# Side work of an expert stream: four lanes with gaps and a VectorE allowance, norms scaled on ScalarE, choices block by block

## The chip, the core and the metric

One core of a Trainium2 chip. The time is that of the device, in microseconds (us), for one execution of the whole kernel. The engines are TensorE (PE in the profile), VectorE (DVE), ScalarE (ACT), GpSimd (POOL) and SyncE (SP), which here only issues DMAs. Each engine executes its own instructions in their order.

## What is computed

Everything is float32; x has four sequences of 1024 rows of 256. The reference, cut to its frame:

```python
x = x + attention(layernorm(x))      # 16 heads, rotary, q and k normed, (q.k)**4, causal
x = x + ffn(layernorm(x))
x = x + silu(conv(layernorm(x)))     # long convolution along the axis of the 4 sequences: 4 taps
x = x + ffn(layernorm(x))            # the same weights again

def ffn(x):
    shared = (silu(x @ g) * (x @ u)) @ w2s                 # inner width 352
    probs = softmax(x @ gate_w.T)                          # 16 experts
    weights, chosen = top_k(probs, 6)
    return shared + sum(weights[k] * expert[chosen[k]](x)) # inner width 176
```

## The kernel before

All of x stays in SBUF as `X`, eight blocks of 128 positions by four sequences. The blocks form two groups of four. A first part does attention, and in its second half the routing of group 0. Then an expert stream runs in four stages: group 0 and group 1 through the first feed-forward layer, then the same through the second. A stage streams 111 tiles, each of 128 rows that one expert takes; which expert it is stands in `table`.

Around a stage lie two steps on GpSimd, both of indirect DMAs with 128 rows each, 96 per group and layer. The *scatter* (`scatter`, L421) writes the normed rows (`sxn`) into a queue in DRAM (`xq`), at places that `plan` worked out. The stage loads the queue three tiles at a time (`xg`, L1001), and stores its results in a second queue (`yq`, L1064). The *combine* (`combine`, gathers at L1147) fetches them back into `yg`, and VectorE adds them to `X`, weighted with the softmax's values `top` (L1131).

One tile of the stream is: `turn` (TensorE transposes the rows, `pxt`, L1014; ScalarE copies them to `xgT`, L1016), `gate_up` (L1030; ScalarE's silu L1038 and VectorE's product L1039 give `hbuf`), `turn_h` (L1044, L1046) and `down` (L1053; ScalarE copies `py` to `yo`, L1062). `stream` writes them out so that one round of its loop holds `gate_up` of tile c, `turn_h` of c - 2, `turn` of c + 2 and `down` of c - 3. After `down` it calls the stage's function with the number of the tile.

That function hands out side work. A piece of side work is a generator that yields "el" or "pe" ahead of a portion (a bite; "pe" ones use TensorE) or "gap" (wait for the next round). `Bites` keeps lanes of such generators, and `step` runs so many bites of each lane. The order is fixed when the program is built, since TensorE, VectorE, ScalarE and SyncE are scheduled by hand; GpSimd's instructions stay in the order in which they were written. In the stream there are three lanes, and gaps are skipped:

- QUEUE: the combine of the previous stage's group, one pair of gathers a tile; when it and SIDE are empty, the scatter for the next stage (one a tile in stage 0, every eighth tile two; two a tile in stages 1 and 2). Each scatter is made to follow the last copy of `hT` written before it.
- SIDE: of each block that the combine completed, `convolve` (norm, four taps, silu, sum), `prepare` (norm, logits) and, after the fourth block, `plan` (softmax, the best eight, one-hot `hot` and its sum `mask`, places `sloti`, and `table` by way of `le` and `ex`). Stage 0 has `prepare` and `plan` of group 1, without `convolve`.
- FILL: the shared expert of the stage's group (28 bites, one every fourth tile).

If a stage's rows are wanted while its scatter is unfinished, `force` drains all side work ahead of them:

```python
def run():
    settle()
    if st not in filled:
        bites.add(QUEUE, fill(st, 2))
        settle()
```

Stage 3 combines group 0 for the last time, three gathers every second tile. After the stream, a tail combines group 1 in triples, each with one bite of the shared expert, and stores the blocks.

Of the kernel before, what the change touches and what calls it, by code (L numbers as in the profile page):

```python
# [8 lines left out]
FP = mybir.dt.float32  # L9
# [15 lines left out]
P = 128  # L25
# [19 lines left out]
class Bites:  # L45
# [4 lines left out]
    def __init__(self, lanes, gaps=True):  # L50
        self.lanes = [[] for _ in range(lanes)]
        self.gaps = gaps

    def add(self, lane, gen, key=None):
        self.lanes[lane].append([key, gen, None])
        self.advance(lane, -1)

    def advance(self, lane, at):
        item = self.lanes[lane][at]
        item[2] = next(item[1], None)  # L60
        while item[2] == "gap" and not self.gaps:
            item[2] = next(item[1], None)
        if item[2] is None:
            self.lanes[lane].pop(at)
# [13 lines left out]
    def step(self, pe, counts):  # L78

        for lane, n in enumerate(counts):  # L80
            for _ in range(n):
                kind = self.kind(lane)
                if kind in (None, "gap") or (kind == "pe" and pe <= 0):
                    break
                if kind == "pe":
                    pe -= 1
# [17 lines left out]
def block_kernel(  # L104
# [25 lines left out]
    rt2 = ctx.enter_context(tc.tile_pool(name="rt2", bufs=2))  # L130
    dram = ctx.enter_context(tc.tile_pool(name="dram", bufs=1, space=bass.MemoryType.DRAM))
# [39 lines left out]
    iota_i = rt.tile([P, NTILE], I32, name="iota_i")  # L171
    nc.gpsimd.iota(iota_i, pattern=[[1, NTILE]], base=0, channel_multiplier=0)
    iota_f = rt.tile([P, NTILE], FP, name="iota_f")
    nc.vector.tensor_copy(iota_f, iota_i)
    iota_e = iota_f[:, 0:NEXP]
    row0 = rt.tile([1, NTILE], FP, name="row0")
    nc.vector.tensor_scalar_mul(row0, iota_f[0:1, :], float(P))
# [8 lines left out]
    def ln_stats(xs, mv, tag):  # L186

        st = small.tile([P, 4, 6], FP, tag=f"st_{tag}", name="ln_st")
        for i in range(4):
            nc.vector.bn_stats(st[:, i, :], xs[:, i, :])  # L190
        for i in range(4):
# [5 lines left out]
    def ln_apply(xs, dst, mv, rstd, n=4):  # L197

        for i in range(n):
# [3 lines left out]
                mv[:, i, 0:1],  # L203
                rstd[:, i : i + 1],
                ALU.subtract,
                ALU.mult,
            )
# [44 lines left out]
    mvs = [rt.tile([P, TT, 2], FP, name=f"mvs{g}") for g in range(NG)]  # L252
    rstds = [rt.tile([P, TT], FP, name=f"rstds{g}") for g in range(NG)]
    plans = {}
    logits = {}
    scatters = [0]

    def prepare(g, i, pool, ps):

        t = g * TG + i  # L260
        xs = X[:, t, :, :]
        mv, rstd = mvs[g][:, 4 * i : 4 * i + 4, :], rstds[g][:, 4 * i : 4 * i + 4]
        yield "el"
        if i == 0:
            logits[g] = rt.tile([P, TT, NEXP], FP, name="lg")
        lg = logits[g]
        ln_stats(xs, mv, "r")
# [5 lines left out]
        nc.vector.reciprocal(rstd, rstd)  # L273
        xn = pool.tile([P, 4, E], FP, tag="rxn", name="rxn")
        ln_apply(xs, xn, mv, rstd)
        xT = pool.tile([P, 2, 512], FP, tag="rxT", name="rxT")
        yield "gap"
        yield "gap"
        for k in range(2):
# [4 lines left out]
        yield "gap"  # L284
# [11 lines left out]
        nc.vector.tensor_copy(lg[:, 4 * i : 4 * i + 4, :], pl)  # L296

    def plan(g, ps):

        yield "el"  # L300
        lg = logits[g]
        sh3 = [P, TT, NEXP]
        mx = small.tile([P, TT], FP, tag="mx", name="mx")
        nc.vector.tensor_reduce(mx, lg, AX.X, ALU.max)
        nc.vector.tensor_sub(lg, lg, mx[:, :, None].to_broadcast(sh3))
        yield "gap"
        yield "el"
        nc.scalar.activation(lg, lg, AF.Exp)
        yield "gap"
        yield "el"  # L310
        sm = small.tile([P, TT], FP, tag="smx", name="smx")
        nc.vector.tensor_reduce(sm, lg, AX.X, ALU.add)
        nc.vector.reciprocal(sm, sm)
        nc.vector.tensor_mul(lg, lg, sm[:, :, None].to_broadcast(sh3))

        top = rt2.tile([P, TT, 8], FP, name="top")
        idx = rt.tile([P, TT, 8], U32, name="idx")
        for c in range(0, TT, 8):
            yield "el"
            for i in range(c, c + 8):  # L320
                nc.vector.max(top[:, i, :], lg[:, i, :])
            for i in range(c, c + 8):
                nc.vector.max_index(idx[:, i, :], top[:, i, :], lg[:, i, :])
        yield "el"
        chosen = rt.tile([P, TT, TOPK], FP, name="chosen")
        nc.vector.tensor_copy(chosen, idx[:, :, 0:TOPK])
        hot = rt.tile([P, TT, TOPK, NEXP], FP, name="hot")
        sh4 = [P, TT, TOPK, NEXP]
# [6 lines left out]
        yield "el"  # L335
        mask = rt.tile([P, TT, NEXP], FP, name="mask")
        nc.vector.tensor_reduce(mask, hot.rearrange("p t k n -> p t n k"), AX.X, ALU.add)

        mf = mask.rearrange("p t n -> p (t n)")
        yield "gap"  # L340
        yield "gap"
        yield "pe"
        pa = ps().tile([P, TT, NEXP], FP, tag="m", name="pa")
# [4 lines left out]
        nc.vector.tensor_copy(tot[:, :, 0:TT], pa.rearrange("p t n -> p n t"))  # L348
        cnt = small.tile([P, NEXP], FP, tag="cnt", name="cnt")
# [19 lines left out]
        yield "el"  # L369
        nc.vector.tensor_mul(hot, hot, at[:, :, None, :].to_broadcast(sh4))  # L370
# [950 lines left out]
```

## Time and profile before

| | us |
|---|---|
| median of 3 runs (2469.45 to 2477.04) | 2473.38 |
| the profiled execution | 2393.24 |
| its span, first to last instruction | 2391.5 |
| TensorE busy in it | 2114.5 (88%) |
| VectorE / ScalarE / GpSimd busy | 1118.5 / 1240.2 / 901.4 |
| granted TensorE clock, mean | 0.925 |

The first `yo` of the stages start at 862.0, 1179.1, 1583.6 and 1989.7 us, the last `yo` of all at 2260.1. The page's slices are 59.8 us each; a digit gives the tenths of a slice in which the engine was busy. A row of waits names the instruction that waited, what it waited for, the sum in us, how often, and the longest. A row of the timeline has start, length, engine, line and operands, and in brackets the idle time ahead of it with what ended it. A row of windows has for each engine the busy time and the instructions in that stretch; when asked for one line of the kernel, only for that line's.

### The profile page before, as it was taken

To read this page: it belongs to the slowest core of one execution; us is meant where nothing else is said; L and a number is where in the kernel's file an instruction comes from. 1 tells how busy PE (TensorE), PEld (TensorE's weight loads), DVE (VectorE), ACT (ScalarE), POOL (GpSimd) and SP (SyncE) were. 2 spreads that over 40 slices of the span, in tenths; PEclk is the share of its full clock that TensorE was granted. 3 is DMA by queue.
4 is the path that set the end of the run, shared out by engine and by line. 5 is a ranking of instruction groups with operands and counts; after the bars stand their busy time and mean duration, and the time that the engine had idled before them with its cause. 6 is when DMAs were issued, how large, how long until landed. Compare 5 with 4: busy or idle time off the path is not lost.

```text
span 2391.5 us, 33033 instructions
## 1 busy us (share of the span) xinstructions
PE 2114.5 (88%) x10480; PEld 1308.4 (55%) x10480; DVE 1118.5 (47%) x2532; ACT 1240.2 (52%) x2754; POOL 901.4 (38%) x990
## 2 busy tenths in 40 slices
PE   5899999778898998999899999789999959999974
PEld 2344443222233466777666667567676747777632
DVE  5888867656555225111166652126754212441154
ACT  3677878566676145555455544335553424555410
POOL 3333211344431000444355226645513654540176
PEclk8888988889888999999999999989999979999987
DMA  7900000111101412555455335344423535663243
GB/s 232 342 7 1 1 1 1 38 51 45 53 27 62 114 48 79 165 166 166 137 151 154 102 104 176 132 139 142 145 92 121 176 124 154 202 186 115 91 123 112
DMA packets 212231, 267.73 MB, mean 112 GB/s; under 512 B 25280, under 2 KB 187232, under 8 KB 212064
## 3 DMA queue, kind: packets, MB, share of 16 engines
q1 hardware_dynamic: 166944, 161.04, 21.6%
q0 software_dynamic: 36992, 100.78, 13.4%
q10 hardware_dynamic: 8128, 3.80, 0.7%
q8 instruction: 91, 1.49, 0.3%
q14 instruction: 76, 0.62, 0.1%
HBM read 123.72 MB, written 141.82 MB: 111 GB/s over the span
## 4 chain that ended last, share of the span: by engine, by line
PE 67%; DVE 12%; issue 7%; ACT 7%; POOL 5%; DMA 2%; ACTq 0%; POOLq 0%; DVEq 0%; SPq 0%
PE pgu L1030 20%; PE py L1053 14%; PE ps L694 6%; PE acc L742 4%; PE pxt L1014 4%; PE pht L1044 4%; POOL xq L421 3%; PE pg L955 3%; ACT s L705 3%; PE pj L571 3%; PE pu L955 3%; PE po L972 3%; POOL yg L1147 2%; ACT s L863 1%; DVE X L1131 1%
## 5 line engine op out<-in xcount | busy, mean ns | idle before, releaser
L421 POOL DMA_INDIRECT xq<-sxn,sloti x384 | 379.2, 987 | 644.7 <-ACT xgT L1016 306.2
L1030 PE MATMUL pgu<-wgu,xgT 128*128 x1776 | 609.7, 466 | 4.4 <-DVE hbuf L1039 2.2
L1147 POOL DMA_INDIRECT yg<-yq,sloti x384 | 375.8, 979 | 421.8 <-issue 201.4
L1039 DVE TENSOR_TENSOR hbuf<-hbuf,pgu 128x176 f32<-128x176 f32 x444 | 149.4, 337 | 721.7 <-ACT hbuf L1038 721.2
L1030 PEld LDWEIGHTS pgu<-wgu,xgT 128*128 128x128 f32 x1776 | 338.7, 193 | 136.5 <-issue 20.3
L1038 ACT ACTIVATE hbuf<-pgu 128x176 f32<-128x176 f32 x444 | 141.4, 318 | 411.7 <-PE pgu L1030 411.6
L705 ACT ACTIVATE s<-ps 128x1024 f32<-128x1024 f32 (+3 forms) x384 | 291.4, 815 | 114.6 <-PE ps L694 113.5
L1053 PE MATMUL py<-w2a,hT 128*128 x888 | 268.7, 385 | 0.9 <-ACT yo L1062 0.9
L1053 PE MATMUL py<-w2b,hT 128*128 x888 | 266.4, 382 | 0.0
L1062 ACT COPY yo<-py 128x256 f32<-128x256 f32 x444 | 166.1, 374 | 167.0 <-PE py L1053 166.7
L1131 DVE SCALAR_TENSOR_TENSOR X<-yg,top,X 128x256 f32<-128x256 f32 x384 | 186.0, 484 | 87.8 <-DMA yg<-yq,sloti 81.8
L1014 PE MATMUL pxt<-ident,xg 128*128 128x128 f32 x888 | 171.8, 276 | 60.6 <-DMA xg<-xq 60.6
L714 POOL TENSOR_SCALAR_AFFINE_SELECT s<-s 128x256 f32<-128x256 f32 x128 | 84.2, 659 | 349.7 <-ACT s L705 349.5
L725 DVE TENSOR_TENSOR s<-s 128x1024 f32<-128x1024 f32 (+3 forms) x160 | 168.2, 1051 | 86.8 <-ACT s L705 83.5
L1016 ACT COPY xgT<-pxt 128x256 f32<-128x256 f32 x444 | 167.9, 378 | 68.7 <-PE pxt L1014 68.3
L694 PE MATMUL ps<-q,kA 32*128 32x512 f32 (+3 forms) x1024 | 182.0, 647 | 20.0 <-ACT s L705 18.0
L1044 PEld LDWEIGHTS pht<-ident,hbuf 128*128 128x128 f32 x888 | 125.9, 142 | 124.4 <-issue 71.1
L1053 PEld LDWEIGHTS py<-w2b,hT 128*128 128x128 f32 x888 | 170.2, 192 | 23.5
L863 ACT ACTIVATE s<-s 128x1024 f32<-128x1024 f32 x192 | 164.4, 856 | 27.5 <-POOL s L714 27.2
L1044 PE MATMUL pht<-ident,hbuf 128*128 128x128 f32 x888 | 171.6, 275 | 4.9 <-ACT hT L1046 4.9
L1046 ACT COPY hT<-pht 128x256 f32<-128x256 f32 x444 | 165.4, 372 | 1.7 <-PE pxt L1014 0.7
L742 PE MATMUL acc<-s,vA 128*32 128x512 f32 (+3 forms) x1024 | 140.1, 603 | 13.2 <-ACT s L863 10.8
(158 smaller groups left out, 2421.9 us busy)
## 6 DMA issues: line engine op xcount, KB each, us to landing
xg<-xq SPq DMA_DIRECT2D x148, 384.0 KB, 3.7
yq<-yo SPq DMA_DIRECT2D x148, 384.0 KB, 2.8
xq<-zero SPq DMA_DIRECT2D x74, 384.0 KB, 4.6
xq<-sxn,sloti POOLq DMA_INDIRECT x384, 2.4
yg<-yq,sloti POOLq DMA_INDIRECT x384, 2.9
wgu<-in_w SPq DMA_DIRECT2D x4, 1408.0 KB, 17.8
X<-in_x SPq DMA_DIRECT2D x8, 512.0 KB, 5.5
out<-X SPq DMA_DIRECT2D x8, 512.0 KB, 3.5
```

The source lines that it names most:

```text
L421: d = nc.gpsimd.indirect_dma_start(out=xq[g][:, :], out_offset=bass.IndirectOffsetOnAxis(ap=sloti[:, c + i, k : k + 1], axis=0), in_=xs[:, ...
L694: nc.tensor.matmul(tiles[h // 2][:, h % 2, 0:nq], lhsT=kt[32 * h : 32 * h + 32, (j % 4) * P : (j % 4 + 1) * P], rhs=qT[u, hf][a][32 * h : ...
L705: nc.scalar.activation(s2[:, :, 0:nq], tiles[pr][:, :, 0:nq], AF.Square)
L725: nc.vector.tensor_mul(part, part, part)
L742: nc.tensor.matmul(acc[32 * r : 32 * r + 32, n0:512], lhsT=va[:, j % 4, h * VW : h * VW + 32], rhs=s2s[r // 2][:, r % 2, 0 : 512 - n0], st ...
L863: nc.scalar.activation(part, part, AF.Square)
L1014: nc.tensor.transpose(pt[:, k, :], xg[c][:, k * P : (k + 1) * P], ident)
L1030: nc.tensor.matmul(pg, lhsT=xT[c][:, k, :], rhs=wgu_f[k][:, bass.ds(vals[0] * (2 * FI), 2 * FI)], start=(k == 0), stop=(k == 1),)
L1044: nc.tensor.transpose(pt[:, k, :], hbuf[c % 4][:, k * P : (k + 1) * P], ident)
L1053: nc.tensor.matmul(py, lhsT=hT[c][:, k, :], rhs=w2_f[k][:, bass.ds(off[c] * E, E)], start=(k == 0), stop=(k == 1),)
L1131: nc.vector.scalar_tensor_tensor(X[:, t, l, :], yg[:, k, :], top[:, i, k0 + k : k0 + k + 1], X[:, t, l, :], op0=ALU.mult, op1=ALU.add,)
L1147: nc.gpsimd.indirect_dma_start(out=yg[:, k, :], out_offset=None, in_=yq[g][:, :], in_offset=bass.IndirectOffsetOnAxis(ap=sloti[:, i, k0 + ...
```

## The change

- `Bites` keeps the gaps in the stream, too. A bite may carry a VectorE time in us; a `step` has an allowance (`room`), and a bite with a time isn't begun once it is used up. Overdraft carries over to the next step, what is left over does not.
- There are four lanes: QUEUE, CONV (convolutions of a group's blocks), CHOOSE (norm, logits and choice of each block, then the plan) and FILL. The stage's function is called twice a tile, before and after `down`, with an allowance of 1.2 each. CONV and CHOOSE share one square root for a block's first norm and the previous block's second.
- Norms in the stream are applied as scale and shift by ScalarE (`ln_apply_act`): for `hxn`, `rxn`, `hn` and `sxn`. In the attention part they stay on VectorE.
- The best eight, `hot` and `mask` are worked out block by block in `choose`, from the logits; the softmax follows after the plan. `table` comes from one comparison with a number per partition and a matmul with the identity.
- The scatter starts when the plan has its places: two a tile in stage 0, three a tile in stages 1 and 2.
- The combine goes in pairs with four buffers everywhere (`f4`), in stages 1 and 2 three pairs in two tiles; also in the tail, where each pair has one bite of the shared expert.
- `hbuf` has three buffers instead of four.

```diff
 class Bites:
-    def __init__(self, lanes, gaps=True):
+    def __init__(self, lanes):
         self.lanes = [[] for _ in range(lanes)]
-        self.gaps = gaps
+        self.room = 0.0
...
-    def step(self, pe, counts):
+    def step(self, pe, counts, room=1e9):
+        self.room = room + min(self.room, 0.0)
         for lane, n in enumerate(counts):
             for _ in range(n):
                 kind = self.kind(lane)
                 if kind in (None, "gap") or (kind == "pe" and pe <= 0):
                     break
+                time = self.lanes[lane][0][3]
+                if time > 0 and self.room <= 0:
+                    break
+                self.room -= time
...
+    def ln_scale_shift(mv, rstd, shift):
+        nc.vector.reciprocal(rstd, rstd)
+        nc.vector.scalar_tensor_tensor(
+            shift, mv[:, :, 0], -1.0, rstd, op0=ALU.mult, op1=ALU.mult
+        )
...
+    def ln_apply_act(xs, dst, rstd, shift, lo, hi):
+        for i in range(lo, hi):
+            nc.scalar.activation(
+                dst[:, i, :],
+                xs[:, i, :],
+                AF.Identity,
+                scale=rstd[:, i : i + 1],
+                bias=shift[:, i : i + 1],
+            )
...
+    def choose(g, i, xn, pool, ps):
...
-        nc.vector.tensor_copy(lg[:, 4 * i : 4 * i + 4, :], pl)
+        nc.vector.tensor_copy(lg, pl)
+        yield ("el", 1.7)
+        idx = small.tile([P, 4, 8], U32, tag="idx", name="idx")
+        for l in range(4):
+            nc.vector.max(top[:, l, :], lg[:, l, :])
+        for l in range(4):
+            nc.vector.max_index(idx[:, l, :], top[:, l, :], lg[:, l, :])
+        yield ("el", 1.5)
...
+        nc.vector.tensor_reduce(mask, hot.rearrange("p t k n -> p t n k"), AX.X, ALU.add)
...
     def plan(g, ps):
...
+        le = small.tile([P, NEXP], FP, tag="le", name="le")
+        nc.vector.tensor_scalar(le, run[:, :, 0], row0, None, ALU.is_le)
+        ex = small.tile([P, 1], FP, tag="ex", name="ex")
+        nc.vector.tensor_reduce(ex, le, AX.X, ALU.add)
...
+        nc.tensor.matmul(px[0:1, :], lhsT=ex, rhs=ident, start=True, stop=True)
...
-        for c in range(0, NTILE, 37):
-            yield "el"
-            le = rt.tile([1, 37, NEXP], FP, name="le")
...
-    def scatter(g, pool, n):
+    def scatter(g, pool, n, act):
...
-            ln_apply(X[:, t, l : l + 2, :], xs, mvs[g][:, c : c + 2, :], rstds[g][:, c : c + 2], 2)
+            if act:
+                ln_apply_act(src, xs, *norm, 0, 2)
+            else:
+                ln_apply(src, xs, *norm, 2)
...
-        hbuf = [fw.tile([P, 2 * P], FP, name=f"hbuf{i}") for i in range(4)]
+        hbuf = [fw.tile([P, 2 * P], FP, name=f"hbuf{i}") for i in range(3)]
...
                 if c >= 3:
+                    st, i = tiles[c - 3]
+                    stages[st][3](i, 0)
                     down(c - 3)
-                    st, i = tiles[c - 3]
-                    stages[st][3](i)
+                    stages[st][3](i, 1)
...
+        def blocks(g, before, conv):
+            summed, known, rooted = set(), set(), set()
...
+            def convolutions():
+                for i in range(TG + 1):
...
+                        while i not in before:
+                            yield "gap"
+                        for lo in (0, 2):
+                            yield ("el", 1.1)
+                            ln_stats(xs, mv[:, 0], lo, lo + 2)
+                    while has[1] and i - 1 not in known:
+                        yield "gap"
+                    yield "gap"
+                    yield "el"
+                    part = slice(0 if has[0] else 1, 2 if has[1] else 1)
+                    nc.scalar.activation(
+                        rs[:, part], mv[:, part, :, 1], AF.Sqrt, bias=eps_t
+                    )
...
+            def choices():
...
+                    yield from choose(g, i, xn, f1, ps_f)
+                yield from plan(g, ps_f)
...
-            for i in range(TT):
-                for k0 in range(0, TOPK, n):
-                    yield "el"
-                    yg = f3.tile([P, n, E], FP, tag="yg", name="yg")
+            for i in range(TT):
+                for k0 in range(0, TOPK, 2):
+                    yield ("el", 1.0)
+                    yg = f4.tile([P, 2, E], FP, name="yg")
...
-                    if len(pending) > 2:
+                    if len(pending) > 3:
                         use()
...
-        QUEUE, SIDE, FILL = range(3)
-        bites = Bites(3, gaps=False)
+        QUEUE, CONV, CHOOSE, FILL = range(4)
+        bites = Bites(4)
...
+            def each(i, at):
+                if i == 0 and at == 0:
+                    begin()
+                to = st + 1
+                if to < 4 and to not in sending and planned[to % NG] > to // NG:
+                    if not bites.lanes[QUEUE]:
+                        sending.add(to)
+                        bites.add(QUEUE, fill(to, 3 if st else 2))
+                n = 1 if at == 0 or (i % 2 and 0 < st < 3 and not sending) else 0
+                bites.begin()
+                bites.step(1, (n, 3, 3, 0), 1.2)
+                if at == 1 and i % 4 == 1:
+                    bites.step(2, (0, 0, 0, 1))
...
-            bites.add(QUEUE, combine(1, 3, last))
+            bites.add(QUEUE, combine(1, last))
             while bites.lanes[QUEUE]:
-                bites.step(9, (1, 0, 1))
+                bites.step(9, (1, 0, 0, 1))
```

## The prediction

> **What bounds the kernel now.** I read the page's slices first, then TensorE's waits, then single stages by window and timeline. TensorE is busy in 2114.5 of 2391.5 us, so what can be won is in its 277 us of idle time, and only where it idles on the path.
>
> ```profile
> PE   5899999778898998999899999789999959999974
> PEclk8888988889888999999999999989999979999987
> POOL 3333211344431000444355226645513654540176
> ...
> PE pxt L1014 <- DMA xg<-xq: 60.6, 3, 25.7
> PE acc L742 <- ACT s L863: 45.0, 30, 6.4
> ...
> PE fpt L182 <- DVE rxn L200: 13.1, 12, 2.1
> PE pa L344 <- DVE mask L337: 13.1, 3, 4.4
> ```
>
> The largest wait occurs three times: the first expert tile of stages 1, 2 and 3 waits for its rows (`xg`), which can't be loaded until the last of 96 scatters (`xq`, L421) has landed. The two dips in the PE row (slices 26 and 33) are stages 2 and 3. The timeline around stage 2 shows it:
>
> ```profile
> 1526.96 0.96 POOL L421 DMA_INDIRECT xq<-sxn,sloti  x1 [3.48 <-ACT xgT L1016]
> 1528.22 0.96 POOL L421 DMA_INDIRECT xq<-sxn,sloti  x1 [0.30 <-issue]
> 1529.49 0.96 POOL L421 DMA_INDIRECT xq<-sxn,sloti  x1 [0.30 <-ACT xgT L1016]
> ...
> 1558.51 0.96 POOL L421 DMA_INDIRECT xq<-sxn,sloti  x1 [0.31 <-issue]
> 1560.97 0.89 SPq L1001 DMA_DIRECT2D xg<-xq  x2
> 1564.40 0.29 PEld L1014 LDWEIGHTS pxt<-ident,xg 128*128 128x128 f32 x2 [25.89 <-issue]
> ```
>
> Two numbers to keep: back to back, a scatter costs GpSimd 0.96 + 0.30 = 1.267 us; and 18 of them stood undone when TensorE needed the rows. The pace of the stream is the distance between two evictions of `py`:
>
> ```profile
> 1527.34 0.37 ACT L1062 COPY yo<-py 128x256 f32<-128x256 f32 x1 [0.38 <-PE py L1053]
> 1529.82 0.37 ACT L1062 COPY yo<-py 128x256 f32<-128x256 f32 x1 [0.38 <-PE py L1053]
> ```
>
> A bare tile is 2.486 us. With the shared expert spread over the stage, the evictions of tiles 70 to 100 of stage 1 stand 90.9 us apart: 3.03 us a tile; I use 3.1. The end of the program is another matter: from 2264 to 2384 us GpSimd issues the last 96 gathers (`yg`) without a break.
>
> **What the change removes.** (a) *The three late starts.* Counted in the changed program's order, the scatters stand at tiles 16 to 63 of stage 0 and 60 to 91 of stages 1 and 2; before, they stood at 24 to 105 and 66 to 105, with the last 4, 18 and 18 forced out at tile 105. At 1.267 us, 96 take 122 us; begun at tile 60 they end near tile 60 + 122/3.1 = 99, before the first rows are wanted at 105. So the wait goes whole. Its price is more than 60.6 us: the last ten evictions of stages 0, 1 and 2 span 36.3, 62.2 and 62.1 us, where ten undisturbed ones span 24.9, 31.7 and 31.7; that is 11.4 + 30.5 + 30.4 = 72.3 us. The other 11.7 us are the pipeline's refill and the clock: after the stall, four `pgu` matmuls take 2.55 us instead of 1.35. The Trainium skill (TensorE: Matmul & The Clock Gate, on the HAM clock gate) gives half rate after an idle window and about 3.4 us to come back, so 1.7 us lost a stall, 5 us in three and a gain of 66. The trace has cold matmuls for nearly 6 us; I take its 72.
>
> (b) *Routing's bursts.* Choosing block by block, with gaps ahead of TensorE's parts, removes the wait for `mask` (4.4 us in each of stages 0, 1, 2; its 2.7 us reduction becomes four small ones) and most of that for `rxn` (13.1 us). Of 26 us I take 20: VectorE may still be late.
>
> (c) *Small VectorE work.* The 12 `le` and 12 `ex` instructions (13.6 + 9.1 us) become two short ones a plan. Under the stream they hide behind TensorE; in the attention part they precede the first scatter, behind which a mask waits on GpSimd, then ScalarE's second square, then `acc` (longest wait 6.4 us). I take 3 of that. Scatters there start nine steps later and still end before the last step; they and the rest of attention stay.
>
> **What it moves.** 192 norm applications (`hxn` 64, `rxn` 48, `hn` 32, `sxn` 48) go from VectorE (0.416 us each) to ScalarE. There no row of this form exists; 128x1024 from SBUF to SBUF takes 1.056 us, 128x256 from PSUM 0.374. I take 0.42: 81 us over four stages and the tail, on a ScalarE that a bare tile uses for 1.44 of 2.486 us (0.378 + 0.372 + 0.374 + 0.318). Against it, ScalarE's table loads fall from 52 to 34, which is 18 x 1.283 = 23 us. This is cost nothing, hidden by TensorE; if that cover failed, 58 us would show. The logits' and combine's smaller extra instructions (shift, one transpose of `ex`) hide likewise. The third `hbuf` instead of a fourth waits for nothing: its reader is one tile past.
>
> **What it adds: two stretches at GpSimd's pace.** (d) *Combine, 48 pairs in 32 tiles.* Before, one pair a tile; now 1.5 in stages 1 and 2. That asks 3 gathers a tile of 3.1 us. A gather's own rate first: in stage 1, 96 take 96.39 us (1.004 each); in stage 3, 91.12 (0.949).
>
> ```profile
> 1180.00:1350.00 170.00, 96.39 (x96) 0.99 0.52 151
> ...
> 1978.00:2150.00 172.00, 91.12 (x96) 1.00 0.62 189
> ```
>
> The skill's GPSIMD Engine Reference (Specifications) says that GpSimd shares its SBUF interfaces with VectorE and contends when VectorE reads two inputs there, as the convolution does. Rule and row have one direction, and the row limits it: 0.055 us a gather, not a multiple. With 0.30 between, 1.30 us each, 2.6 a pair; 2.5 without contention. Pair 0 starts about 2 us into the stage (3.6 us after the last `yq` store, as 2260.46 to 2264.09) and lands 4.15 us later (second gather 1.25, landing 2.9). Pair p is thus usable at 6.2 + 2.6p; VectorE meets its use with pair p + 3. The last met in the stretch is pair 44 at tile 31: ready at 120.6, asked for at 31 x 3.1 = 96. VectorE stands 24.5 us late; behind it queue the `hbuf` products, for which TensorE's `pht` waits. About two tiles of lead (5 us) absorb some: 19 us a stage. Bounds: 6 (3.3 us a tile as routing adds work, 2.5 a pair, 8 us of lead: 116 - 102 - 8) and 25 (no lead).
>
> (e) *Scatter, 3 a tile*: 3.8 us of GpSimd in 3.1. The norms `sxn` are now on ScalarE with two buffers; the one at tile 86 (26 tiles after the start) overwrites the pair whose last scatter is the 72nd: landed at 71 x 1.267 + 2.4 = 92.4, asked for at 80.6. Behind ScalarE's wait stand `yo`, `hT`, `xgT`, so TensorE stops after about 2 us: 10 us a stage; bounds 0 and 14. In stage 0, two a tile, the same reckoning leaves room: nothing. If GpSimd ends late, the stage's end has tiles 99 to 105 as cover.
>
> (f) *The tail.* The shared expert's 28 parts now accompany 28 pairs (70 us) instead of 28 triples (105 us). The same four blocks alone took 20.9 us each at 773 to 857: 84 us. VectorE's uses then wait behind TensorE, GpSimd for its four buffers, whose slack is some 5 us: 0 to 13, taken as 5.
>
> **Sum**, against the profiled 2391.5 us span (2393.2 with what lies around it): -72 - 20 - 3 + 38 + 20 + 5 = -32, so 2359. The runs' median is 2473.4, 80 us above the profiled execution, without a trace that shows why; I carry the difference over in proportion: -33, **2440 us** (1.3% faster). Single stage: 404.5 - 30.5 - 8 + 29 = 395 us.
>
> **The rivals.** *Pace absorbed* (chance 0.23): the lead of `hbuf` and `xgT` and the low bounds hold, so 58 shrinks to 12: -78, 2393 us. For it: ScalarE and VectorE are half idle. Against: both are in order, and nothing lets GpSimd issue sooner. *It doesn't do what it says* (0.09): three scatters and three gathers a tile don't happen, since TensorE falls back to GpSimd's pace and loses there what it won at the ends. With both stretches at their high bounds (78), (b) at half and the tail at 5 to 13 that is -2 to +6: 2471 to 2480. *Slower* (0.14): GpSimd's price per row. 90 gathers and 72 scatters a stage lie on the stretches, so 0.10 us more each costs 16 us a stage and the gain is gone; that is 1.40 us a gather. The longest single gather row is 1.69 us, so contention can reach it, and more VectorE work than before falls beside the gathers. At 0.2 us more: +65 on -32, 2507 us. Against: the row's mean moved only 0.055 beside the same convolution. The forecast itself has 0.54, with 2410 to 2466 as its own range.
>
> **How the numbers follow.** Within 0.3% is about what a measurement of this kernel can tell from no change. Faster: the forecast's 0.54 and 0.23, 0.77. Same: 0.09. Slower: 0.14. For 8 in 10 the range reaches half into the absorbed case and just over no change: 2390 to 2480; all low bounds together (-72 - 26 - 5 + 12) would give 2379, all high ones (-72 + 78 + 13) 2493.
>
> **What would show it.** Right: no wait of `pxt` for `xg` over 1 us; stage 1 from first to next first eviction near 395 us; VectorE's wait for `yg` in the first 32 tiles of stages 1 and 2 (8.6 us in stage 1 before) above 30 us; ScalarE waiting for scatters at `sxn`; table loads at 34. Wrong: a GpSimd row clearly above 1.0 us; TensorE waiting for `hT` or `xgT` outside those stretches, so that the moved norms aren't hidden; a tail well over 131 us.

## The result, and the profile after

The changed kernel takes **2590.9 us** (median of 4 runs, 2584.0 to 2594.7) where the kernel before takes 2474.0 us (2469.5 to 2477.0): ratio 1.0459, 95% interval 1.0441 to 1.0478, so 4.6% slower. The forecast was 2440 us, and the range, 2390 to 2480, does not hold it. The profiled execution is one of those runs: span 2589.2 us.

The page of the changed kernel, its slices (tenths of busy time in 40 slices of the span):

```profile
PE   5898989777778988899779887977998798899980
PEclk8889988877789999999889989988999898999995
POOL 3333211434420026501560166066116605620166
```

The two dips where TensorE stood at the stages' ends are gone. Instead it stands at 7 in six slices of the stages (from the 14th slice on), and each of the six is one in which GpSimd's row is at 5 or 6. The largest waits of TensorE, each in us in total, times, longest:

```profile
PE pht L1085 <- ACT hT L1087: 52.6, 26, 6.2
PE acc L786 <- ACT s L907: 51.2, 25, 6.5
PE py L1094 <- ACT yo L1103: 45.8, 38, 3.7
PE py L1094 <- issue: 29.9, 19, 3.0
...
PE pxt L1055 <- issue: 18.4, 15, 2.8
```

The wait of `pxt` for `xg` (60.6 us before) is no longer there, as forecast. New are waits for ScalarE's copies `hT` and `yo`. Is ScalarE too slow? The timeline of the last stage, where neither routing nor the shared expert runs, says no (start, duration, engine, instruction, idle time before it and what ended it):

```profile
2214.72 0.38 PE L1085 MATMUL pht<-ident,hbuf 128*128 128x128 f32 x2
2214.94 0.38 PE L1055 MATMUL pxt<-ident,xg 128*128 128x128 f32 x2
...
2215.18 0.32 ACT L1079 ACTIVATE hbuf<-pgu 128x176 f32<-128x176 f32 x1 [1.07 <-PE pht L1085]
...
2215.59 0.59 PE L1094 MATMUL py<-w2b,hT 128*128 x2
...
2216.69 0.37 ACT L1087 COPY hT<-pht 128x256 f32<-128x256 f32 x1 [1.20 <-PE py L1094]
...
2218.12 0.37 ACT L1057 COPY xgT<-pxt 128x256 f32<-128x256 f32 x1 [1.06 <-PE pht L1085]
...
2219.49 0.37 ACT L1103 COPY yo<-py 128x256 f32<-128x256 f32 x1 [0.99 <-PE pxt L1055]
```

TensorE has finished `pht` at 2215.10, `pxt` at 2215.32 and `py` at 2216.18. ScalarE stands idle and still starts the copies of these three results at 2216.69, 2218.12 and 2219.49, one release each 1.4 us. What these copies wait for is a counter that TensorE raises; the trace has its rises at 2215.16, 2216.61, 2218.05, 2219.47 and 2220.90, and then two more within 0.1 us. The price of a row did not move: a scatter has a mean of 993 ns, a gather of 981 (987 and 979 before).

What is late is the count by which an engine tells the others that an instruction is done; I follow TensorE's. 2701 matmuls raise it, and the trace keeps most of its rises. I call a matmul *late* if no rise is recorded within 0.5 us of its end: 1 in the profile of before, 471 in this one. (By the same rule ScalarE has 1 and 315, VectorE 0 and 214, so it is not TensorE's count alone.) Some of TensorE's rises (203 here) are missing from the record, so "late" in such a sum means late or unrecorded. I also read the trace without them: the `yo` copies that start over 0.5 us after both the end of `py` and ScalarE's own previous instruction. Of those that start within 3 us after the start of an indirect transfer by GpSimd, that is 0 of 304 in the profile of before and 49 of 205 in the profile of after; of the others, 0 and 2.

### The profile page after: what moved, and what is told of

Read it like the earlier page. It is cut to its first block, busy times and chain, and to the rows that moved or that the text cites. A ratio compares the mean times of both kernels' runs of the same rounds, so it can differ in the third digit from the quotient of the medians.

```text
span 2589.2 us, 33065 instructions
## 1 busy us (share of the span) xinstructions
PE 2179.5 (84%) x10488; PEld 1327.9 (51%) x10488; DVE 1042.3 (40%) x2405; ACT 1300.7 (50%) x2923; POOL 905.5 (35%) x991
## 4 chain that ended last, share of the span: by engine, by line
PE 55%; another core or an unknown queue 4%; issue 4%; ACT 4%; DVE 2%; POOL 1%; DMA 0%; ACTq 0%; DVEq 0%
PE pgu L1071 20%; PE py L1094 16%; PE pxt L1055 4%; PE pht L1085 4%; PE pg L996 3%; PE po L1013 3%; PE pu L996 3%; PE pl L331 1%; ACT yo L1103 1%; ACT rxn L229 1%; POOL yg L1282 1%; PE hpt L192 1%; PE fpt L192 0%; ACT xgT L1057 0%
## 5 line engine op out<-in xcount | busy, mean ns | idle before, releaser
L1071 PE MATMUL pgu<-wgu,xgT 128*128 x1776 | 627.2, 477 | 0.9 <-issue 0.7
L1071 PEld LDWEIGHTS pgu<-wgu,xgT 128*128 128x128 f32 x1776 | 348.3, 198 | 139.1 <-issue 25.7
L1094 PE MATMUL py<-w2a,hT 128*128 x888 | 287.7, 407 | 76.8 <-ACT yo L1103 45.8
L1094 PE MATMUL py<-w2b,hT 128*128 x888 | 275.3, 393 | 0.0
L1085 PE MATMUL pht<-ident,hbuf 128*128 128x128 f32 x888 | 177.6, 283 | 64.6 <-ACT hT L1087 52.6
L1055 PE MATMUL pxt<-ident,xg 128*128 128x128 f32 x888 | 177.7, 283 | 23.3 <-issue 18.4
L1087 ACT COPY hT<-pht 128x256 f32<-128x256 f32 x444 | 165.9, 374 | 52.6 <-PE py L1094 19.6
L1094 PEld LDWEIGHTS py<-w2a,hT 128*128 128x128 f32 x888 | 140.0, 198 | 96.1 <-ACT yo L1103 57.5
L1094 PEld LDWEIGHTS py<-w2b,hT 128*128 128x128 f32 x888 | 175.7, 198 | 26.1
```

The costliest lines, as they stand in the source:

```text
L1055: nc.tensor.transpose(pt[:, k, :], xg[c][:, k * P : (k + 1) * P], ident)
L1071: nc.tensor.matmul(pg, lhsT=xT[c][:, k, :], rhs=wgu_f[k][:, bass.ds(vals[0] * (2 * FI), 2 * FI)], start=(k == 0), stop=(k == 1),)
L1085: nc.tensor.transpose(pt[:, k, :], hbuf[c % 3][:, k * P : (k + 1) * P], ident)
L1087: d = nc.scalar.copy(hT[c], pt)
L1094: nc.tensor.matmul(py, lhsT=hT[c][:, k, :], rhs=w2_f[k][:, bass.ds(off[c] * E, E)], start=(k == 0), stop=(k == 1),)
```

## The experiments

**The kernel before, profiled again.** Its first profile lay 80 us below its runs. No edit.

> The kernel before, unchanged, for a second profile. Its recorded execution was 2393 us, its timed runs 2469 to 2477. Theory L (counts of finished work reach the waiting engine late while GpSimd issues indirect transfers, in most executions of either kernel): 2473 us, and the profile now shows hundreds of TensorE counts that rise over 0.5 us after the matmul's end (1 in the first profile, 471 in the changed kernel's), with tiles of the last stage that have gathers beside them above the 24.9 us for ten. Theory C (the change itself brings the late counts): 2473 us with fewer than 10 late counts, and the 80 us stand elsewhere.

2480.5 us, ratio 1.0007 (0.9993 to 1.0021), span 2479.7. Theory L holds for it: 333 late matmuls. All of them are among the 1541 that end within 6 us after the start of an indirect transfer, none among the other 1160. So the kernel before has it too, and its first profile must come from a place without it. The runs below met such a place: one chip on which the kernel before takes 2393 us (twice, 55 and 39 runs, and there the late matmuls number 0 to 3 in every profile). On the four other sets of runs it takes 2474 to 2478 us, with 313 to 497 late ones in every profile of a kernel. I call the one chip clean and the others late. Each comparison is with the kernel before on its own chip.

**The changed kernel again, on two more chips.** No edit.

> The changed kernel, unchanged, for a second measurement. Two chips have been seen: on one the kernel before takes 2478 us and its TensorE counts rise late in hundreds of cases, on the other it takes 2393 us and none is late. Chip theory: on a chip of the first kind 2590 us (ratio 1.046); on one of the second kind, where the changed kernel with a sparser last stage took 2394 us, 2393 to 2402 us, no change. If the loss belonged to the change alone, the ratio would be 1.046 on either.

> The changed kernel, unchanged, once more. Chip theory: on a chip where the kernel before takes about 2393 us, 2393 to 2402 us, ratio 1.000 to 1.004 (its last stage at most 2 us above the 270.3 us of the bare pace). On a chip where the kernel before takes about 2478 us, 2590 to 2605 us again.

2603.1 us (ratio 1.0530, 1.0497 to 1.0563) and 2609.3 us (1.0542, 1.0487 to 1.0597). Both were late chips, so the loss repeats, and the changed kernel itself was never run on the clean one.

**GpSimd's old rate.**

```diff
-                        bites.add(QUEUE, fill(to, 3 if st else 2))
+                        bites.add(QUEUE, fill(to, 2 if st else 1))
-                n = 1 if at == 0 or (i % 2 and 0 < st < 3 and not sending) else 0
+                n = 1 if at == 0 else 0
```

> The changed kernel with GpSimd's old rate: one pair of gathers a tile in all stages, two scatters a tile in stages 1 and 2, one in stage 0. If the rate of GpSimd's transfers per tile is what costs, stages 1 and 2 fall back from 461 and 455 us to about 420 and the run to about 2500 us. If the number of transfers counts, and not how densely they stand, each stage stays within 10 us and the run at 2580 to 2600 us.

2523.1 us, ratio 1.0185 (1.0151 to 1.0218), on a late chip. Stage 0 falls from 326 to 316 us, stage 1 from 464 to 430, stage 2 from 457 to 433 (from the first eviction of a stage to that of the next). These are the values of the kernel before, although its late starts are back as well: the last ten evictions of the three stages span 40.8, 60.7 and 61.4 us again, where the changed kernel has 24.9, 33.5 and 33.5. So the density cost the changed kernel more than the falls show, some 61 us in stage 1 (34 + 27). The number of transfers is the same, so the density counts. The last stage, whose rate the edit leaves alone, stays at 315 us (275.5 before the change).

**Two suspects on the engines.** The norms back on VectorE:

```diff
-            nc.scalar.activation(
+            nc.vector.tensor_scalar(
                 dst[:, i, :],
                 xs[:, i, :],
-                AF.Identity,
-                scale=rstd[:, i : i + 1],
-                bias=shift[:, i : i + 1],
+                rstd[:, i : i + 1],
+                shift[:, i : i + 1],
+                ALU.mult,
+                ALU.add,
             )
```

> The changed kernel with every norm that it moved back on VectorE (one instruction of multiply and add instead of ScalarE's). If the moved norms fill ScalarE, whose copies TensorE waits for, the 192 of them at about 0.42 us or more give back 50 to 80 us: about 2520 us. If they are hidden, as the prediction had it, the run stays at 2580 to 2600 us or gets longer.

and a fourth hidden buffer:

```diff
-        hbuf = [fw.tile([P, 2 * P], FP, name=f"hbuf{i}") for i in range(3)]
+        hbuf = [fw.tile([P, 2 * P], FP, name=f"hbuf{i}") for i in range(4)]
-                h = hbuf[c % 3]
+                h = hbuf[c % 4]
```

> The changed kernel with four buffers for the expert's hidden rows instead of three. The largest wait of TensorE after the change is that for hT, 52.6 us. If a late release of the third buffer is behind it, 20 to 50 us come back: 2540 to 2570 us. If three are enough, as the prediction had it, 2585 to 2597 us.

On one late chip 2616.4 us (ratio 1.0557, 1.0525 to 1.0589) and 2607.5 us (1.0515, 1.0472 to 1.0558). The changed kernel takes 2590.9 to 2609.3 on late chips, so neither gives anything back. The moved norms and the third buffer are not the loss.

**The rate alone, on the kernel before.** In the last stage only:

```diff
-            bites.step(1, (1 if i % 2 == 0 else 0, 0, 0))
+            bites.step(1, (1 if i % 3 < 2 else 0, 0, 0))
```

> The kernel before with one edit: in the last stage the triples of gathers accompany two tiles in three, so 2 gathers a tile as in the changed kernel, instead of 1.5. Density theory: the last stage grows from 275 to 300 to 315 us, the run to about 2510 us. Form theory: 275 to 280 us, the run unchanged. By GpSimd's pace alone, without late counts, 96 x 1.25 to 1.30 = 120 to 125 us over 48 tiles that take 119: at most 6 us.

> The kernel before with the last stage's gathers at 2 a tile instead of 1.5, again. Without late counts it took 2394 us, the same as the kernel before. On a chip with late counts, density theory: last stage 300 to 315 us instead of 275, run about 2510 us; form theory: 275 to 280 us.

On the clean chip 2394.4 us, ratio 1.0009 (1.0000 to 1.0019), last stage 272.3 us. On a late chip 2519.0 us, ratio 1.0176 (1.0140 to 1.0212), last stage 318.6 us. One kernel, one stretch of 96 gathers, in the view by window (sum; PE, PEld, DVE, ACT, POOL busy with instructions; TensorE's clock; DMA share; GB/s). The clean chip, up to the 93rd gather:

```profile
1991.00:2111.00 120.00, 118.83 (x569) 90.27 (x569) 55.49 (x137) 61.22 (x189) 90.47 (x93) 1.00 0.71 216
```

The late chip:

```profile
2050.00:2223.00 173.00, 143.65 (x603) 102.29 (x602) 60.36 (x146) 64.49 (x201) 92.50 (x96) 0.91 0.52 160
```

TensorE is busy in 99% of the first and in 83% of the second. GpSimd works the same 0.97 us a gather in both (90.47 / 93, 92.50 / 96). VectorE and ScalarE are about half idle or more. TensorE's matmuls are longer, 0.238 us each instead of 0.209 (143.65 / 603, 118.83 / 569), at a granted clock of 0.91 instead of 1.00: some 18 us. The other 28 us are more idle time (29.35 against 1.17). A slower clock of that chip is not the cause, since it would not leave TensorE idle, and once the gathers are over the same execution runs without a break at 1.00:

```profile
2223.00:2350.00 127.00, 127.00 (x614) 97.54 (x614) 17.21 (x51) 66.05 (x205) 0.00 (x0) 1.00 0.34 108
```

So what tells the two apart is the waiting between the engines, and the clock drops where TensorE waits.

**Grouping, and pauses.** The changed kernel with pairs in three tiles of four in the last stage (the second edit is the evenly spread version below with one in two):

```diff
                 n = 1 if at == 0 or (i % 2 and 0 < st < 3 and not sending) else 0
+                if st == 3 and i % 4 == 3:
+                    n = 0
```

> The changed kernel with one edit: in the last stage the pairs of gathers accompany three tiles in four, so that GpSimd has 1.5 gathers a tile there, as before the change, still in pairs. Density theory (late counts cost when GpSimd issues nearly without a pause): the last stage falls from 310 to 270 to 285 us, the run to about 2560 us. If the form (pairs, four buffers, the third hidden buffer, the place ahead of the down product) is what costs, the stage stays at 305 to 315 us.

> The evenly spread version, with the last stage's pairs at one in two tiles (1 gather a tile) instead of three in four (1.5). On a chip with late counts the last stage was 293 us there; density theory: 272 to 280 us, run about 2455 us, ratio to the kernel before about 0.99. If any indirect transfer costs the same wherever it stands: 290 us and more. On a chip without late counts: 2358 us, unchanged.

Both met the clean chip: 2394.0 us (ratio 1.0008, 1.0000 to 1.0017) and 2358.4 us (0.9862, 0.9842 to 0.9883), the last stage at 270.3 us in both, the bare pace. (What the second gains over the first comes from the even spread, below.) The same settings of that stage are in other runs on late chips, which gives a table of the last stage alone (us, 96 gathers each; the triples are in the kernel before, the pairs in the changed one):

| gathers a tile | grouping | clean chip | late chips |
|---|---|---|---|
| 1 | a pair each second tile | 270.3 | 273.1 |
| 1.5 | a triple each second tile (before) | 270.3 | 275.5 |
| 1.5 | a pair in three tiles of four | 270.3 | 293.5, 293.5 |
| 2 | a pair each tile (after) | not run | 310.0, 312.2, 312.1 |
| 2 | a triple in two tiles of three | 272.3 | 318.6 |

The same 96 gathers cost 3 to 46 us on a late chip, by how they stand. The mean rate is not all of it (293.5 against 275.5), so my density theory is too simple: at equal rate, triples with a whole tile of pause did better than pairs with shorter ones. The two kernels also differ in their buffers and in where the gathers stand beside `down`, so the grouping alone is not shown to do it. Three of the five late rows rest on one execution each, on different chips.

**Whose lateness?** The gathers of the last stage as plain transfers of the same size by SyncE, which take the rows in order instead of the chosen ones, and, in another kernel, the gathers kept and VectorE's multiply-adds of that stage left out:

```diff
+                        if direct:
+                            r = (i * TOPK + k0 + k) * P
+                            nc.sync.dma_start(out=yg[:, k, :], in_=yq[g][r : r + P, :])
+                            continue
                         nc.gpsimd.indirect_dma_start(
```

```diff
-                for k in range(2):
+                for k in range(0 if leave else 2):
                     nc.vector.scalar_tensor_tensor(
```

> The changed kernel with the last stage's 96 gathers replaced by plain transfers of the same size from the same rows in order, issued by SyncE (so the last stage combines the wrong rows). If GpSimd's issuing of indirect transfers delays the counts: the last stage is 270 to 276 us, with fewer than 10 late counts in it; the run about 2555 us. If the transfers themselves do (their traffic, or VectorE's waits for them), it stays above 295 us.

> The changed kernel with the last stage's 96 gathers replaced by plain transfers of the same size issued by SyncE (the last stage combines the wrong rows), again: the first time it ran on a chip without late counts, where nothing was to be seen. On a chip with late counts: if GpSimd's issuing delays them, the last stage is 270 to 278 us instead of 310 and the run about 2560 us; if the transfers or VectorE's waits for them do, it stays above 295 us. On a chip without: 2395 us.

> The changed kernel with the 96 multiply-adds of the last stage's combine left out (VectorE then waits for no gathered row there; the gathers are still issued, and the outputs of that half lack the experts' part). On a chip with late counts: if VectorE's waits for gathered rows are the path, the last stage falls from 310 to below 285 us; if the late counts between TensorE, ScalarE and VectorE are, it stays at 300 us or more. On a chip without: 270 us, as with them.

All three met the clean chip: 2395.3 us (ratio 1.0005, 0.9994 to 1.0016), 2394.9 us (1.0013, 1.0005 to 1.0021) and 2395.0 us (1.0014, 1.0004 to 1.0024), the last stage 270.3 us each time. So they don't tell whether GpSimd's issuing or the transfers' traffic delays the counts. What they do give is the changed kernel's other stages on the clean chip, three times, and the last stage with a pair of gathers each tile whose rows nobody waits for: nothing above the bare pace.

The profiles from late chips give a hint. In eleven of them, 414 of 2499 `yo` copies started over 0.5 us late where their inputs were ready within 1.25 us of the start of an indirect transfer (GpSimd executes one for 0.97 us); 20 of 147 did between 1.25 and 2 us, 1 of 103 between 2 and 3, and none of 2135 beyond. Of the packets of a scatter that stands alone, about a third start between 2 and 3 us. And from 50 to 100 us of the kernel before on its late chip, plain transfers move 341 GB/s, more than twice the 160 above, with no late matmul. That speaks for the issuing and against traffic as such, but it is no test.

**Spread evenly.** The changed kernel with gathers and scatters set as thin as the stage ends allow:

```diff
+                n = 1 if at == 0 else 0
+                if at == 0 and sending:
+                    n = (2 if i % 4 == 0 else 1) if st == 0 else (3 if i % 2 else 2)
+                if st == 3 and i % 4 == 3:
+                    n = 0
...
-                        bites.add(QUEUE, fill(to, 3 if st else 2))
+                        bites.add(QUEUE, fill(to, 1))
```

> The changed kernel with GpSimd spread evenly: one pair of gathers a tile in stages 1 and 2 and three in four tiles in the last, scatters at 1.25 a tile in stage 0 and 2.5 in stages 1 and 2 from about tile 65, so that they end near tile 103, ahead of the first rows of the next stage. Density theory: stages 1 and 2 near 405 us (the late start of 28 us gone, less what 2.5 a tile cost), the last near 277, stage 0 near 310: run 2430 to 2460 us, below the kernel before. If the late starts come back in another form, 2490 us or more.

> The evenly spread version again. On a chip without late counts 2358 us, as before. On a chip with them: density theory 2440 to 2470 us, below the kernel before there (2478), since no stretch runs GpSimd without pauses; if the late counts cost per transfer and not per density, 2490 us or more.

Clean: 2358.1 us, ratio 0.9862 (0.9846 to 0.9878). Late: 2472.0 us, ratio 0.9976 (0.9963 to 0.9989). Against the changed kernel on the same late chip (2603.1) that is 131 us, by order and spacing alone; against the changed kernel's relatives on the clean chip (2394.0 to 2395.3) it is some 36. The time on the late chip lies 2 us above the range that was expected, and its last stage at 293.5 us instead of 277.

**The attention part.** It had grown on every chip. Two edits on the evenly spread version. First, the scatters earlier, with the rest of the plan (table and weights) after them:

```diff
-                        bites.add(ROUTE, chain(plan(0, ps_m), scatter(0, ap2, 1, False)))
+                        bites.add(
+                            ROUTE,
+                            chain(
+                                chain(plan(0, ps_m, True), scatter(0, ap2, 1, False)),
+                                plan_rest(0, ps_m),
+                            ),
+                        )
```

> The evenly spread version with one edit in the attention part: the scatter of the first half starts as soon as its slots are known, and the table and the weights of that half are worked out after it, so that the scatters stand five steps earlier in GpSimd's order. If the later start of the scatters costs the 14 to 20 us by which the attention part grew, 5 to 12 us come back there (first eviction of the stream near 868 instead of 875 to 885 us). If it is the clock or other side work, nothing.

2482.1 us, ratio 1.0027 (1.0011 to 1.0043), where the version it starts from took 2472.0 on the same chip; the first eviction is at 893.4 instead of 883.5 us. Earlier was worse: a miss. The scatters now stand in front of more masks: ScalarE's wait for them, the one shown below, is 54.1 us in 11 times. Then half of the scatters moved behind attention, beside the shared expert's blocks (with the sparser last stage):

```diff
-                        bites.add(ROUTE, chain(plan(0, ps_m), scatter(0, ap2, 1, False)))
+                        bites.add(ROUTE, chain(plan(0, ps_m), scatter(0, ap2, 1, False, 0, 8)))
...
             bites.add(FILL, shared_all(0))
-            bites.drain(FILL)
+            bites.add(QUEUE, scatter(0, f2, 2, True, 8, TT))
+            while bites.lanes[FILL]:
+                bites.begin()
+                bites.step(9, (1, 0, 0, 1))
+            bites.drain(QUEUE)
```

(and one scatter in four steps instead of two before that).

> The version of m_slow3, with half of the first half's scatters (48 of 96) taken out of the attention part and issued beside the shared expert's four blocks that stand between attention and the first expert tile, where GpSimd does nothing: 48 x 1.27 = 61 us in 84. If the scatters cost the attention part (behind them wait its masks on GpSimd), 10 to 20 us come back: first eviction near 865 instead of 875 to 885 us. If the shared blocks have no cover for them, or the scatters aren't what costs, 0 to -5 us.

> The version with half of the first scatters beside the shared blocks, again. On a chip without late counts 2321 us, as before (ratio 0.971). On a chip with them: the evenly spread version took 2472 us there with a last stage of 293; the sparser last stage gives 13 to 20 us and the attention part 20 to 35: 2420 to 2440 us, ratio 0.976 to 0.985.

Clean: **2321.5 us, ratio 0.9709** (0.9689 to 0.9729), first eviction at 846.1 us. Late: **2432.1 us, ratio 0.9815** (0.9761 to 0.9868), 861.2 us. The scatters do cost the attention part: without half of them it is 39 us shorter on the clean chip than in the version with the sparser last stage (884.8). A part of why is seen in ScalarE's wait for the masks that GpSimd writes between its scatters, on the clean chip from 440 to 760 us, which holds all the scatters of either kernel there. Before:

```profile
ACT s L863 <- POOL s L714: 27.2, 8, 8.3
```

The evenly spread version, whose attention part is the changed kernel's:

```profile
ACT s L907 <- POOL s L758: 44.5, 7, 11.2
```

With half of the scatters gone:

```profile
ACT s L907 <- POOL s L758: 18.6, 5, 8.5
```

17 us more of this wait stand against 13 to 25 us that the part grew. TensorE's granted clock goes with it: from 500 to 700 us it is 0.87 before, 0.78 in the evenly spread version and 0.86 with half of the scatters gone. How the growth divides between wait and clock was not separated. In GpSimd's order the first scatters before the change come in groups of 5, 4, 3 and 12 with a mask after each; in the changed kernel as 1, one mask, and then 23 in a row, which is 29 us at 1.267 us each, with four masks behind.

## Why the prediction was wrong

The parts of the span, in us: attention up to the first eviction, the stages from first to next first eviction (the last to its last), and the tail. The clean chip's column of the changed kernel is from the three relatives whose edits touch the last stage alone; its last stage is the least that the bare pace allows.

| | before, clean | changed, clean | before, late | changed, late |
|---|---|---|---|---|
| attention | 862.0 | 882 to 885 | 871.9 | 885.9 |
| stage 0 | 317.0 | 300.3 | 316.8 | 326.5 |
| stage 1 | 404.5 | 402 to 404 | 428.7 | 463.8 |
| stage 2 | 406.2 | 402 to 406 | 433.4 | 457.0 |
| stage 3 | 270.3 | 270.3 and up | 275.5 | 310.0 |
| tail | 131.4 | 131 to 133 | 153.5 | 146.0 |
| span | 2391.5 | 2389 to 2398 | 2479.7 | 2589.2 |

**The step that failed for the measured time is the last one of the sum**: "I carry the difference over in proportion". The 80 us between the runs and the profile were not a constant of the chip. They go with late counts beside indirect transfers, stage by stage: 24, 27 and 22 us of the 88 in stages 1, 2 and the tail, 0 in stage 0 with its one scatter a tile (first against third column). The change packs these transfers closer, and on a late chip the price rises from 88 to about 195 us (second against fourth column: 26, 60, 53, 40 and 14 us from stage 0 on). The gap between profile and runs was the one thing in the data that no row explained, and it should have widened the range. Instead it was scaled. Why late counts cost some chips and not others stays open; that they lie where GpSimd's indirect transfers are dense, and grow when these are packed closer, is shown.

**On the clean chip the sum missed as well**: -32 forecast, about 0 measured on the relatives. By its steps:

- (a) *Late starts*: right. Stage 0 lost 16.7 us where 11.4 and about a third of (b) were forecast. The last ten evictions of stages 1 and 2 span 33.5 us instead of 62.2 and 62.1.
- (b) *Routing's bursts*: partly. The wait for `mask` fell from 13.1 to 3.7 us, but that for `rxn` stayed (16.4 us in the clean run with the sparser last stage, now for ScalarE), and a wait of `px` for `ex`, 10.4 us, is new. The 20 us were too many.
- (c) *Attention stays*: wrong, by 25 us on the clean chip: -3 forecast, about +22 measured. I named the chain (mask, ScalarE's second square, `acc`) and the nine steps' delay and priced only the delay. What grew is ScalarE's wait for masks behind scatters (27.2 to 44.5 us) and the time at a lower clock (0.87 to 0.78).
- (d) and (e) *Combine and scatter at GpSimd's pace*: the mechanism is right where counts are on time. The waits in stage 1 of the clean run with the sparser last stage, VectorE's from 1183 to 1290 us (combine), ScalarE's from 1380 to 1530 us (scatter):

```profile
DVE X L1266 <- DMA yg<-yq,sloti: 38.4, 42, 3.0
```

```profile
ACT sxn L229 <- DMA xq<-sxn,sloti: 7.8, 3, 5.3
```

Both were forecast (over 30 us; ScalarE waiting at `sxn`). The size was forecast at 29 us a stage. The evenly spread version, with one pair and 2.5 scatters a tile, has stages of 385.2 and 385.7 us on the clean chip, 16 to 20 below the relatives, though its last ten evictions take 4 to 5 us longer; I estimate the two stretches at 20 to 25 us a stage from that. In the changed kernel's own profile, on a late chip, VectorE's wait in these tiles (1212 to 1314 us) is 5.0 us, and the sign is absent; that the late counts held the stream back first there is my reading, and not shown.

- The last stage was counted at nothing. Two gathers at 1.25 us in a tile of 2.49 leave GpSimd no pause at all. I overlooked that as a stretch at GpSimd's pace. On the clean chip the price would be about 2 us (from the triples at the same rate), on late ones it is 35 to 37 (310.0 to 312.2 against 275.5).
- (f) *Tail*: +5 forecast. 0 to 1.6 on the clean chip, and on late ones it got shorter (153.5 to 146).

**The rivals.** *Pace absorbed* (2393) is near the 2394 to 2395 of the clean chip's relatives by chance only: it stood for 78 us less than the profiled 2391.5, which is 2313 there, and the relatives gain nothing. The pace was not absorbed (20 to 25 us a stage), and attention ate the rest of the gain. *Slower, by GpSimd's price per row* had the right side and the right place (what lies beside dense gathers and scatters) and the wrong price: the row stayed at 0.98 to 0.99 us, while the price was paid by counts between other engines. Its 2507 us fall short of 2591. Of the signs of being wrong, TensorE's waits for `hT` came (52.6 us), and the tail at 146.0 is well over 131, but the norms back on VectorE gave nothing, and the kernel before has 153.5 on a late chip. Of those of being right: no `pxt` wait for `xg` was right; stage 1 near 395 us was 402 to 404 on the clean chip and 464 on the late one; table loads are 34, as forecast.

## What to carry to other kernels

If timed runs and the profile differ by 3%, find where before forecasting a change: a second profile of the same kernel showed it stage by stage, and showed that the surplus belonged to exactly what the change would make denser. On such chips, fine-grained work handed between engines is best kept away from stretches where another engine issues indirect transfers without pauses; the same transfers, thinned, and partly moved under a block of long matmuls, gave 1.8 to 2.9% over the kernel before on both kinds of chip. On an in-order engine that serves two masters (GpSimd: masks and scatters), look at what stands in front of each critical instruction, not only at how many transfers there are.

## What was not expected of the hardware

Two kinds of behaviour of one program on different chips: the kernel before took 2393 us on one and 2474 to 2478 us on the others. On the latter the counts of finished instructions arrive late beside GpSimd's indirect transfers, in the passage shown one release per 1.4 us, and several hundred of TensorE's 2701 in an execution are late or unrecorded; elsewhere in the same execution none is, though plain transfers run there too (in the last 60 tiles of the changed kernel's last stage, for instance). That GpSimd's indirect transfers go with it is shown. Whether their issue, their descriptors or their traffic is the cause, and why one chip is free of it, stays open: the runs meant to tell it all met the clean chip.

The recording itself is a rival that no run excludes. In the same stretches of the late chips the profile loses records: of the counts of landed transfers the kernel before has 19,381 in its first profile and 10,930 in its second. Each timed execution on record comes with its span and clock, so none is known to have run unrecorded; a time without any recording would tell. Also open is why triples with a pause did better than pairs at the same rate.
